# Mamba states by half of the channels, with B and C fetched once per half, and a PSUM bank moved from the state sums to the expert blocks

## The chip, the cores and the metric

The kernel runs on one core of one Trainium2 chip, in one launch. The metric is the device time of the execution in microseconds (us). A core has five engines with a queue of instructions each: PE (TensorE, matrix products), DVE (VectorE), ACT (ScalarE), POOL (GpSimd) and SP (SyncE, which here issues transfers). Each engine works through its queue in order; waits between engines are semaphores. Transfers run on 16 DMA engines. PE writes its results into PSUM, which has eight banks of 512 float32 values per partition.

## The reference, cut to what matters

The input is 16 sequences of 512 tokens with 128 features. Six residual steps follow each other, each on a layer-normalized input: half of an expert layer (8 experts, 2 chosen per token, with a capacity), attention, half of that expert layer again, half of a second expert layer, a Mamba mixer, and half of the second expert layer again.

```
x = x + 0.5 * _L0_ffn_ref(_layernorm(x), ...)
x = x + _L0_attn_ref(_layernorm(x), ...)
x = x + 0.5 * _L0_ffn_ref(_layernorm(x), ...)
x = x + 0.5 * _L1_ffn_ref(_layernorm(x), ...)
x = x + _L1_attn_ref(_layernorm(x), ...)      # Mamba
x = x + 0.5 * _L1_ffn_ref(_layernorm(x), ...)
```

The change touches Mamba's scan. For each of 256 channels d and 16 states n, along the 512 tokens:

```
dA = exp(delta[t, d] * A[d, n])
h  = h * dA + delta[t, d] * B[t, n] * x[t, d]
y[t, d] = sum over n of h[d, n] * C[t, n]
y = (y + D * x) * silu(z), then the product with W_out
```

B and C depend on the token and the state, but not on the channel. An expert block is two products with a GELU between: h = gelu(x W1 + b1), y = h W2 + b2.

## The kernel before, in words

**Layout.** All activations (`x_0` to `x_15`, one tile per sequence) stay in SBUF. The work of the six steps is cut into tasks per sequence or per group of sequences. All arithmetic is float32.

**Expert layers.** A call of an expert layer works on a group of 2 to 5 sequences. `front` normalizes and computes the gate, `routes` chooses experts and slots on DVE, `scatter` writes each token's row to its two slots in DRAM with indirect transfers from POOL, `blocks` runs the experts on blocks of 256 slots, and `back` gathers each token's two results with indirect transfers and adds them. There are 16 calls and 368 blocks. A block is: SP loads the weights `wb` (578 KB, three buffers, L693) and the rows `xs` (128 KB, three buffers, L697); PE transposes the rows into PSUM (`turned`, L709) and DVE or ACT copies them out as `bl_xT` (L712, L714); PE does the first product into two banks `ps_h` (L727); ACT applies the GELU into `hT` (L736); PE does the second product into `ps_b` (L676); DVE adds the bias into `yo` (L681), and the ACT queue issues the store (L685). The second product of a block is issued one block later than its first. Transposes and second products both take their bank from the pool `ps_b`, which holds one.

**Attention.** Two sequences may be in work at a time. For each of four tiles of 128 queries: scores into `ps_a` (two banks), mask and maximum on DVE, exponent on ACT, transposes into `ps_s0` (L867), a copy by ACT (L869), the product with v into `ps_s1` (L872) and the addition into x on DVE (L875). The projection to v also goes into `ps_s1` (L843).

**Mamba.** The 256 channels are two halves (h = 0, 1) of 128 partitions, the 16 states are eight pairs (g). `before` does the projections and convolutions, `delta` makes delta, its product `dx` with x, and writes the rows of B and C to DRAM. `states` runs over g outside and h inside. Once per g, SP loads a pair of rows of B and of C, spread over all partitions (512 KB each, L969; B has two buffers, C three). Then one step per (g, h): DVE multiplies B with `dx` into `u` (L978); for each of the two states ACT computes the exponent into a bank of `ps_a` (L984) and DVE scans along the tokens (L987); POOL multiplies with C (L990); and PE adds the result to the sum of the half, as a product with the identity (L997). The sums of both halves are open over all eight g, in two banks, `ps_s0` and `ps_s1`. `u` has five buffers. There are 16 x 16 = 256 steps. `end` adds D times x to both sums (L1010), multiplies with the gate (L1013), and does the output product (L1017).

**Order.** The program text doesn't set the order of the instructions. A planner at the end of the kernel function first picks among the tasks by ranks and due times, running each to its next `yield`; then `arrange` takes the resulting stream and gives each engine its own order by a list schedule with written-in costs of the instructions and the transfers, the number of buffers in each pool, and the order in which each pool's tiles were asked for. That order is fixed in the built program. A change of buffers therefore moves instructions everywhere.

PSUM is full: `ps_h` 2 banks, `ps_b` 1, `ps_t` 1, `ps_s` 2, `ps_a` 2.

Of the kernel before, what the change touches and what calls it, by code (L numbers as in the profile page):

```python
# [11 lines left out]
F32 = mybir.dt.float32  # L12
I32 = mybir.dt.int32
AF = mybir.ActivationFunctionType
ALU = mybir.AluOpType
AX = mybir.AxisListType
PSUM = bass.MemoryType.PSUM

P = 128
NB, SEQ, D = 16, 512, 128  # L20
NT = SEQ // P
# [6 lines left out]
DI, NH = 256, 2  # L28
NS = 16
RANK = 64  # L30
NCH = 2
# [285 lines left out]
def macaron_kernel(ctx: ExitStack, tc: tile.TileContext, a: dict, out: bass.AP):  # L317
    nc = tc.nc

    def pool(name, bufs, **kw):  # L320
        return ctx.enter_context(tc.tile_pool(name=name, bufs=bufs, **kw))
# [11 lines left out]
    bc_p = pool("bc", 3)  # L333
    s_p = pool("scan", 5)
    dram = pool("dram", 2, space=bass.MemoryType.DRAM)
    ps_h = pool("ps_h", 1, space=PSUM)
    ps_b = pool("ps_b", 1, space=PSUM)
    ps_t = pool("ps_t", 1, space=PSUM)
    ps_s = pool("ps_s", 1, space=PSUM)
    ps_a = pool("ps_a", 2, space=PSUM)  # L340
# [10 lines left out]
    def load(name, src, shape):  # L351
        t = const.tile(shape, F32, name=name)
        nc.scalar.dma_start(out=t, in_=src)
        return t
# [14 lines left out]
    dp = load("dp", a["L1_attn_D_param"], [P, NH])  # L369
# [5 lines left out]
    for e in range(E):  # L375
# [5 lines left out]
        out=tril, in_=ones, compare_op=ALU.is_ge, fill=0.0, base=0, pattern=[[-1, P]],  # L381
# [4 lines left out]
        out=upper, in_=ones, compare_op=ALU.is_gt, fill=0.0, base=0, pattern=[[1, P]],  # L386
# [15 lines left out]
    for g in range(NSLOTS):  # L402
        t = dram.tile([NBLK * BS, D], F32, name=f"slots_{g}", bufs=1)
# [9 lines left out]
    for pre, names in (("L0_ffn_", ("W1", "W2", "b1", "b2")), ("L1_ffn_", ("w1", "w2", "b1", "b2"))):  # L413
        t = dram.tile([P, E, WIDE], F32, name=f"packed_{pre}", bufs=1)
        w1d, w2d, b1d, b2d = (a[pre + n] for n in names)
        at = 0
        for src in (w1d, w2d.rearrange("p e f d -> p e (f d)"), b1d, b2d.unsqueeze(0).to_broadcast([P, E, D])):
            n = src.shape[2]
# [74 lines left out]
    def transpose(src, psum):  # L493

        for j in range(NT):
            nc.tensor.transpose(psum[:, j * P : (j + 1) * P], src[:, j, :], ident)
# [327 lines left out]
    def attention(b):  # L824
        scale = D ** -0.5
        xn = normalized(x[b])
        pt = ps_a.tile([P, SEQ], F32, name="ps_a")
        transpose(xn, pt)
        xT = xT_p.tile([D, PAD + SEQ], F32, name="xT")[:, :SEQ]
        nc.scalar.copy(xT, pt)  # L830
        yield
        qk = []
        both = m_p.tile([P, 2, SEQ], F32, name="a_qk", tag=f"cv{b % 2}")
        for i, n in enumerate("qk"):
            pq = ps_a.tile([P, SEQ], F32, name="ps_a")
            nc.tensor.matmul(pq, wa[n], xT, start=True, stop=True)
            t = both[:, i, :]
            nc.scalar.copy(t, pq)
            qk.append(t)
        q, k = qk  # L840
        pv = ps_s.tile([P, NT, D], F32, name="ps_s1")
        for j in range(NT):
            nc.tensor.matmul(pv[:, j, :], xT[:, j * P : (j + 1) * P], wa["v"], start=True, stop=True)  # L843
        v = m_p.tile([P, NH, SEQ], F32, name="a_v", tag="dx", bufs=2)[:, 0, :].rearrange(
            "p (j d) -> p j d", j=NT
        )
        nc.scalar.copy(v, pv)
        yield
        for i in range(NT):
            n = (i + 1) * P  # L850
            s = ps_a.tile([P, SEQ], F32, name="ps_a")
            nc.tensor.matmul(s[:, :n], q[:, i * P : n], k[:, :n], start=True, stop=True)
            nc.vector.tensor_tensor(s[:, i * P : n], s[:, i * P : n], tril, ALU.mult)

            m = m_p.tile([P, NH, SEQ], F32, name="a_m", tag="zs", bufs=3)[:, 0, :]
            nc.vector.tensor_scalar(m[:, :n], s[:, :n], 0.0, HIDDEN, ALU.is_equal, ALU.mult)
            nc.vector.tensor_tensor(m[:, :n], m[:, :n], s[:, :n], ALU.add)
            g = small.tile([P, 1], F32, name="a_g")
            nc.vector.tensor_reduce(g, m[:, :n], AX.X, ALU.max)
            nc.vector.tensor_scalar(g, g, LEAST, -scale, ALU.max, ALU.mult)  # L860
            pr = m_p.tile([P, NH, SEQ], F32, name="a_p", tag="xc", bufs=3)[:, 0, :]
            z = small.tile([P, 1], F32, name="a_z")
            nc.scalar.activation(pr[:, :n], m[:, :n], AF.Exp, bias=g, scale=scale, accum_out=z)
            nc.vector.reciprocal(z, z)
            pp = ps_s.tile([P, SEQ], F32, name="ps_s0")
            for j in range(i + 1):
                nc.tensor.transpose(pp[:, j * P : (j + 1) * P], pr[:, j * P : (j + 1) * P], ident)  # L867
            pT = m_p.tile([P, NH, SEQ], F32, name="a_pT", tag="dl", bufs=2)[:, 0, :]
            nc.scalar.copy(pT[:, :n], pp[:, :n])  # L869
            po = ps_s.tile([P, SEQ], F32, name="ps_s1")[:, :D]  # L870
            for j in range(i + 1):
                nc.tensor.matmul(  # L872
                    po, pT[:, j * P : (j + 1) * P], v[:, j, :], start=j == 0, stop=j == i
                )
            nc.vector.scalar_tensor_tensor(x[b][:, i, :], po, z, x[b][:, i, :], ALU.mult, ALU.add)  # L875
            yield

    def mamba(b):
# [81 lines left out]
        def states():  # L960


            zs, xc, dl, dx, rows = (st[n] for n in ("zs", "xc", "dl", "dx", "rows"))
            py = []
            for g in range(NS // NCH):
                bc = []
                for n, name in enumerate(("B", "C")):
                    t = bc_p.tile([P, NCH, SEQ], F32, name=name, bufs=2 + n)
                    nc.sync.dma_start(  # L969
                        out=t,  # L970
                        in_=rows[n, g * NCH : (g + 1) * NCH, :]
                        .unsqueeze(0)
                        .to_broadcast([P, NCH, SEQ]),
                    )
                    bc.append(t)
                for h in range(NH):
                    u = s_p.tile([P, NCH, SEQ], F32, name="u")
                    nc.vector.tensor_tensor(  # L978
                        u, bc[0], dx[:, h, :].unsqueeze(1).to_broadcast([P, NCH, SEQ]), ALU.mult
                    )  # L980
                    for i in range(NCH):
                        n = g * NCH + i
                        da = ps_a.tile([P, SEQ], F32, name="ps_a")
                        nc.scalar.activation(  # L984
                            da, dl[:, h, :], AF.Exp, scale=am[:, h, n : n + 1]
                        )
                        nc.vector.tensor_tensor_scan(  # L987
                            u[:, i, :], da, u[:, i, :], 0.0, ALU.mult, ALU.add
                        )
                    nc.gpsimd.tensor_tensor(u, u, bc[1], ALU.mult)  # L990

                    def later(g=g, h=h, u=u):
                        if not py:
                            for n in range(NH):
                                py.append(ps_s.tile([P, SEQ], F32, name=f"ps_s{n}"))
                        for i in range(NCH):
                            nc.tensor.matmul(  # L997
                                py[h],
                                ident,
                                u[:, i, :],  # L1000
                                start=g == 0 and i == 0,
                                stop=g == NS // NCH - 1 and i == NCH - 1,
                            )

                    yield later

            def end():
                ys = xc
                for h in range(NH):
                    nc.vector.scalar_tensor_tensor(  # L1010
                        ys[:, h, :], xc[:, h, :], dp[:, h : h + 1], py[h], ALU.mult, ALU.add
                    )
                nc.vector.tensor_tensor(ys, ys, zs, ALU.mult)  # L1013
                po = ps_t.tile([P, NT, D], F32, name="ps_t")
                for j in range(NT):
                    for h in range(NH):
                        nc.tensor.matmul(  # L1017
                            po[:, j, :],
                            ys[:, h, j * P : (j + 1) * P],
                            wout[:, h, :],  # L1020
                            start=h == 0,
                            stop=h == NH - 1,
                        )
                nc.vector.tensor_tensor(x[b], x[b], po, ALU.add)

            st["end"] = end
# [20 lines left out]
    def of(n, b):  # L1047
        return next(g for g, m in enumerate(moes[n]) if b in m["members"])
# [83 lines left out]
    for b in range(NB):  # L1132
        for n in range(4):
            g = of(n, b)
# [30 lines left out]
    while left:  # L1165
        ready = []
        for name in left:
            t = tasks[name]
# [4 lines left out]
        at, _, name = min((r for r in ready if r[0] <= first + WINDOW), key=lambda r: (r[1], r[0]))  # L1173
        t = tasks[name]
# [59 lines left out]
```

## Time and profile before

| | |
|---|---|
| time, median of 3 runs | 3594.3 us (3581.81 to 3594.71) |
| profiled execution, its own time | 3629.43 us |
| span of the profile | 3627.7 us |
| PE busy | 2802.4 us (77%) |
| DVE busy | 2412.1 us (66%) |
| ACT busy | 2152.2 us (59%) |
| POOL busy | 1855.7 us (51%) |
| moved by DMA | 552.52 MB, mean 152 GB/s |
| mean granted clock of PE | 0.90 |

The profile is one execution. Busy time is the time in which an engine carries out an instruction. A group of instructions is told by its line in the kernel, its engine, its operation, and its tiles as out<-in; behind the bar stand its busy time in us and the mean duration of one in ns, behind the second bar the idle time of the engine just ahead of these instructions, with what ended it. PEld is PE's weight load. SPq is the queue of SP with its transfers. A float32 product shows as two instructions of PE. PEclk is the share of the clock that PE was granted.

### The profile page before, as it was taken

The numbers are of one execution on the slowest core, as the hardware profiler recorded it, in microseconds if no ns is written. First come the engines' busy times: TensorE is split into PE (matmuls) and PEld (weight loads), VectorE is DVE, ScalarE is ACT, GpSimd is POOL, SyncE is SP. The second block draws the span as 40 slices with busy tenths as digits, with TensorE's granted clock in tenths as the row PEclk, the third lists the DMA queues.
The fourth block names the chain that finished last, engine by engine and source line by source line (L and its number), as shares of the span: only waits on it lengthen the run. The fifth ranks groups of instructions, "written<-read, shape, count | busy, mean of one in ns | idle before, by whom it ended". The sixth has DMA issues, their size and how long they took to land. (4 is left out here: it accounts for less than half of the span.)

```text
span 3627.7 us, 45599 instructions
## 1 busy us (share of the span) xinstructions
PE 2802.4 (77%) x13384; PEld 2005.3 (55%) x13384; DVE 2412.1 (66%) x5487; ACT 2152.2 (59%) x3752; POOL 1855.7 (51%) x1557
## 2 busy tenths in 40 slices
PE   3788686776767758887897986789899679854775
PEld 2677575665656645675555652455566256521564
DVE  6714572572662418863798898889788897999512
ACT  2335372552634438873887874789788669842432
POOL 2771504405245343555636468873644984577413
PEclk9999887978889879998999997999999989977888
DMA  9675414414346535654555452455565356433354
GB/s 291 184 215 156 117 58 136 143 52 144 92 124 186 153 104 186 213 161 144 177 177 173 151 182 86 145 175 169 156 192 157 132 174 205 135 115 118 108 169 134
DMA packets 379575, 552.52 MB, mean 152 GB/s; under 512 B 43136, under 2 KB 278336, under 8 KB 379328
## 3 DMA queue, kind: packets, MB, share of 16 engines
q1 hardware_dynamic: 243648, 433.39, 38.8%
q0 software_dynamic: 32768, 67.17, 6.1%
q10 hardware_dynamic: 102912, 49.06, 4.7%
q8 instruction: 107, 1.75, 0.2%
q14 instruction: 140, 1.15, 0.1%
HBM read 448.28 MB, written 110.66 MB: 154 GB/s over the span
## 5 line engine op out<-in xcount | busy, mean ns | idle before, releaser
L990 POOL TENSOR_TENSOR u<-u,C 128x1024 f32<-128x1024 f32 x256 | 640.6, 2506 | 536.5 <-DVE u L987 367.9
L736 ACT ACTIVATE hT<-ps_h,wb 128x256 f32<-128x256 f32 x1472 | 602.4, 474 | 525.9 <-PE ps_h L727 306.6
L676 PE MATMUL ps_b<-wb,hT 128*128 128x128 f32 x5888 | 800.9, 289 | 109.7 <-DVE bl_xT L712 47.8
L676 PEld LDWEIGHTS ps_b<-wb,hT 128*128 128x128 f32 x5888 | 769.2, 203 | 208.9 <-issue 82.0
L727 PE MATMUL ps_h<-bl_xT,wb 128*128 128x256 f32 x2944 | 803.9, 405 | 26.0 <-ACT hT L736 13.8
L775 POOL DMA_INDIRECT gt<-results,whole x512 | 523.8, 1023 | 571.0 <-DVE x L767 171.3
L662 POOL DMA_INDIRECT slots<-row,whole x512 | 532.1, 1039 | 521.8 <-issue 268.6
L997 PE MATMUL ps_s<-u,ident 128*128 128x512 f32 x1024 | 553.3, 659 | 156.2 <-POOL u L990 155.8
L727 PEld LDWEIGHTS ps_h<-bl_xT,wb 128*128 128x128 f32 x2944 | 558.8, 205 | 163.7 <-issue 71.3
L987 DVE TENSOR_TENSOR_SCAN u<-ps_a,u 128x512 f32<-128x512 f32 x512 | 602.8, 1208 | 49.6 <-ACT ps_a L984 43.3
L681 DVE TENSOR_TENSOR yo<-ps_b,wb 128x256 f32<-128x256 f32 x368 | 154.4, 420 | 685.7 <-PE ps_b L676 383.8
L978 DVE TENSOR_TENSOR u<-B,dx 128x1024 f32<-128x1024 f32 x256 | 450.3, 1767 | 31.0 <-PE ps_s L997 18.5
L984 ACT ACTIVATE ps_a<-dl,am 128x512 f32<-128x512 f32 x512 | 345.2, 686 | 197.1 <-DVE u L987 173.4
L997 PEld LDWEIGHTS ps_s<-u,ident 128*128 128x128 f32 x1024 | 192.5, 206 | 362.9 <-POOL u L990 219.7
L709 PE MATMUL ps_b<-ident,xs 128*128 128x128 f32 x736 | 164.0, 298 | 237.8 <-DVE yo L681 167.1
L767 DVE SCALAR_TENSOR_TENSOR x<-gt,m,x 128x128 f32<-128x128 f32 x512 | 228.8, 455 | 80.4 <-DMA gt<-results,whole 69.5
L709 PEld LDWEIGHTS ps_b<-ident,xs 128*128 128x128 f32 x736 | 95.1, 148 | 331.7 <-DVE yo L681 212.2
L907 PE MATMUL ps_t<-xT,wc 128*128 128x512 f32 x512 | 242.3, 611 | 22.6 <-ACT cv L910 9.1
L736 ACT ACT_TABLE_LOAD x176 | 225.8, 1283 | 56.2 <-PE ps_h L727 20.5
L657 POOL TENSOR_SCALAR row<-x,q,off 128x128 f32<-128x128 f32 x256 | 157.7, 618 | 135.2 <-DVE off L564 122.6
L984 ACT ACT_TABLE_LOAD x146 | 187.3, 1283 | 13.9 <-DVE yo L681 5.4
L714 ACT ACTIVATE bl_xT<-ps_b,beta,gamma 128x256 f32<-128x256 f32 x184 | 103.3, 561 | 154.4 <-PE ps_b L709 117.9
(170 smaller groups left out, 2904.5 us busy)
## 6 DMA issues: line engine op xcount, KB each, us to landing
wb<-packed_L_ffn__215 SPq DMA_DIRECT2D x184, 578.0 KB
wb<-packed_L_ffn__222 SPq DMA_DIRECT2D x184, 578.0 KB
B<-rows SPq DMA_DIRECT2D x128, 512.0 KB
C<-rows SPq DMA_DIRECT2D x128, 512.0 KB
xs<-slots SPq DMA_DIRECT2D x368, 128.0 KB
results<-yo ACTq DMA_DIRECT2D x368, 128.0 KB
slots<-empty SPq DMA_DIRECT2D x4, 3456.0 KB
slots<-row,whole POOLq DMA_INDIRECT x512
```

Source lines behind the costliest of these rows:

```text
L662: ins = nc.gpsimd.indirect_dma_start(out=dst, out_offset=bass.IndirectOffsetOnAxis(ap=st["whole"][:, k, i : i + 1], axis=0), in_=row, in_o ...
L676: nc.tensor.matmul(py[:, j, :], hT[:, f, j * P : (j + 1) * P], w2b[:, f, :], start=f == 0, stop=f == NF - 1,)
L709: nc.tensor.transpose(pt[:, j * P : (j + 1) * P], xs[:, j, :], ident)
L727: nc.tensor.matmul(ph[f // 2][:, f % 2, :], w1b[:, f * P : (f + 1) * P], xT, start=True, stop=True)
L736: return nc.scalar.activation(hT[:, f, :], ph[f // 2][:, f % 2, :], act, bias=b1b[:, f : f + 1])
L775: nc.gpsimd.indirect_dma_start(out=gt, out_offset=None, in_=st["results"][: nblk * BS, :], in_offset=bass.IndirectOffsetOnAxis(ap=st["whol ...
L907: nc.tensor.matmul(ph, wc[i][:, h, k, :], xT[:, at : at + SEQ], start=k == 0, stop=k == 3)
L978: nc.vector.tensor_tensor(u, bc[0], dx[:, h, :].unsqueeze(1).to_broadcast([P, NCH, SEQ]), ALU.mult)
L984: nc.scalar.activation(da, dl[:, h, :], AF.Exp, scale=am[:, h, n : n + 1])
L987: nc.vector.tensor_tensor_scan(u[:, i, :], da, u[:, i, :], 0.0, ALU.mult, ALU.add)
L990: nc.gpsimd.tensor_tensor(u, u, bc[1], ALU.mult)
L997: nc.tensor.matmul(py[h], ident, u[:, i, :], start=g == 0 and i == 0, stop=g == NS // NCH - 1 and i == NCH - 1,)
```

## The change

The loops of `states` are turned round: h outside, g inside. B and C are now loaded inside both, so that each pair of rows is loaded once for each half. Only one half's sum is open at a time, in one bank `ps_s`; after the eighth g of a half its D times x is added at once, by the instruction that stood in `end`. Attention's transposes and its product with v share this one bank, and the projection to v takes a bank of `ps_a`. The pool `ps_b` gets the bank that has come free. The buffers of B, C and u are as they were, and so is the arithmetic of each step. The planner, its ranks and the costs are unchanged and give a new order.

```diff
-    ps_b = pool("ps_b", 1, space=PSUM)
+    ps_b = pool("ps_b", 2, space=PSUM)
...
-        pv = ps_s.tile([P, NT, D], F32, name="ps_s1")
+        pv = ps_a.tile([P, NT, D], F32, name="ps_a")
...
-            pp = ps_s.tile([P, SEQ], F32, name="ps_s0")
+            pp = ps_s.tile([P, SEQ], F32, name="ps_s")
...
-            po = ps_s.tile([P, SEQ], F32, name="ps_s1")[:, :D]
+            po = ps_s.tile([P, SEQ], F32, name="ps_s")[:, :D]
...
-            py = []
-            for g in range(NS // NCH):
-                bc = []
-                for n, name in enumerate(("B", "C")):
-                    t = bc_p.tile([P, NCH, SEQ], F32, name=name, bufs=2 + n)
-                    nc.sync.dma_start(...)
-                    bc.append(t)
-                for h in range(NH):
+            py = {}
+            for h in range(NH):
+                for g in range(NS // NCH):
+                    bc = []
+                    for n, name in enumerate(("B", "C")):
+                        t = bc_p.tile([P, NCH, SEQ], F32, name=name, bufs=2 + n)
+                        nc.sync.dma_start(...)
+                        bc.append(t)
                     u = s_p.tile([P, NCH, SEQ], F32, name="u")
...
                     def later(g=g, h=h, u=u):
-                        if not py:
-                            for n in range(NH):
-                                py.append(ps_s.tile([P, SEQ], F32, name=f"ps_s{n}"))
+                        if g == 0:
+                            py[h] = ps_s.tile([P, SEQ], F32, name="ps_s")
...
+                        if g == NS // NCH - 1:
+                            nc.vector.scalar_tensor_tensor(
+                                xc[:, h, :], xc[:, h, :], dp[:, h : h + 1], py[h], ALU.mult, ALU.add
+                            )
...
             def end():
                 ys = xc
-                for h in range(NH):
-                    nc.vector.scalar_tensor_tensor(
-                        ys[:, h, :], xc[:, h, :], dp[:, h : h + 1], py[h], ALU.mult, ALU.add
-                    )
```

More of the change, by code (lines that the diff above doesn't have):

```diff
@@ L963, in states @@
             zs, xc, dl, dx, rows = (st[n] for n in ("zs", "xc", "dl", "dx", "rows"))
-            py = []
-            for g in range(NS // NCH):
-                bc = []
-                for n, name in enumerate(("B", "C")):
-                    t = bc_p.tile([P, NCH, SEQ], F32, name=name, bufs=2 + n)
[L969 to L973, printed above, removed]
-                    )
-                    bc.append(t)
-                for h in range(NH):
+            py = {}
[4 more added lines that the diff above has]
+                        t = bc_p.tile([P, NCH, SEQ], F32, name=name, bufs=2 + n)
+                        nc.sync.dma_start(
+                            out=t,
+                            in_=rows[n, g * NCH : (g + 1) * NCH, :]
+                            .unsqueeze(0)
+                            .to_broadcast([P, NCH, SEQ]),
+                        )
+                        bc.append(t)
                     u = s_p.tile([P, NCH, SEQ], F32, name="u")
@@ L1003, in later @@
                             )
+                        if g == NS // NCH - 1:
+                            nc.vector.scalar_tensor_tensor(
+                                xc[:, h, :], xc[:, h, :], dp[:, h : h + 1], py[h], ALU.mult, ALU.add
+                            )
                     yield later
@@ L1008, in end @@
                 ys = xc
-                for h in range(NH):
-                    nc.vector.scalar_tensor_tensor(
-                        ys[:, h, :], xc[:, h, :], dp[:, h : h + 1], py[h], ALU.mult, ALU.add
-                    )
                 nc.vector.tensor_tensor(ys, ys, zs, ALU.mult)
```

## The prediction

> **What bounds the kernel now.** I read the table of stages first: the busy time of each engine in three stretches, cut at the first and at the last multiply with B (L978 starts at 1381.4 us and ends near 3378).
>
> ```profile
> core 0: us, PE busy (x) PEld busy (x) DVE busy (x) ACT busy (x) POOL busy (x), PEclk, DMA share, GB/s
> 0.00:1330.00 1330.00, 955.52 (x5336) 796.22 (x5337) 659.68 (x2744) 570.77 (x1241) 553.02 (x667) 0.88 0.49 145
> 1330.00:3390.00 2060.00, 1682.96 (x7040) 1067.70 (x7039) 1704.88 (x2587) 1495.63 (x2316) 1239.83 (x822) 0.91 0.50 157
> 3390.00:3628.00 238.00, 163.96 (x1012) 141.33 (x1010) 47.55 (x157) 85.81 (x196) 62.82 (x68) 0.89 0.51 151
> ```
>
> No engine is full in stage 1 (expert blocks and attention): PE leads with 955.52 of 1330 (72%). In stage 2 (Mamba, with expert blocks between) DVE has 83% and PE 82%. Stage 3 is the last 37 expert blocks, where DVE has 20%. The DMA engines stand at half everywhere.
>
> Second, what PE waits for (the view of waits, whole execution):
>
> ```profile
> PE ps_b L709 <- DVE yo L681: 167.1, 106, 11.5
> PE ps_s L997 <- POOL u L990: 155.8, 78, 14.1
> PE ps_b L709 <- issue: 48.6, 18, 17.8
> PE ps_b L676 <- DVE bl_xT L712: 47.8, 22, 10.1
> PE ps_b L676 <- ACT bl_xT L714: 19.7, 16, 5.9
> ```
>
> The columns are total us, times, longest. The first line is the one bank ps_b: the transposes of the next block (L709) wait until DVE has emptied the second product (yo). The fourth and fifth are the same bank the other way round. The second line is not about banks: POOL's product with C is late. By stage, the same view gives L709 for yo 87.7, 55.2 and 24.2 us, and L676 for bl_xT 54.3, 8.3 and 3.0.
>
> Third, the chain of DVE and the tiles B and C. L978, L987 (groups) and then the DMA rates around one pair B, C (40 slices of 0.25 us from 3350; B was issued at 3350.59, C at 3351.01):
>
> ```profile
> L987 DVE TENSOR_TENSOR_SCAN u<-ps_a,u 128x512 f32<-128x512 f32 x512 | 602.8, 1208 | 49.6 <-ACT ps_a L984 43.3
> L978 DVE TENSOR_TENSOR u<-B,dx 128x1024 f32<-128x1024 f32 x256 | 450.3, 1767 | 31.0 <-PE ps_s L997 18.5 <-issue 11.4 <-DMA xs<-slots 0.5
> DMA  0000005898896999889964200000000000007000
> ```
>
> DVE hardly ever waits for B (nothing of the 31.0 us is a B transfer). The pair's data flows from about 3351.5 to 3355.7, so the second of two tiles is there 4.7 us after its issue; one tile alone is half of that flow, some 3.2 us from issue.
>
> **The change, part by part.** The sum is made against the profiled execution, 3629.4 us (span 3627.7 and 1.7 around it); it ran 35.1 us over the median of the runs, 3594.3. I carry the difference over to the median. In the built order the blocks stay where they were (159 before the first state sum, then 172, then 37), so each part can be priced in its own stage. The order of PE does use the bank: transposes stand directly behind a second product 199 times (81 before), and the second products are cut into 686 groups (477).
>
> *Second bank of ps_b, stage 1.* The uses of ps_b alternate, so with two banks transposes always get one and second products the other. A wait of L709 for yo is not wholly removed: after the transposes (0.4 us) and a first product (1.9) PE meets the next second product, and that needs the bank which the same yo must empty. So a wait gives back at most about 2.1 us. The 49 waits of 87.7 us in this stage are mostly below 2 us with a few up to 11.5; cut at 2.1 they hold 50. Cut at 2.0, one second product, the 54.3 us of L676 hold 28. Together 78 us of PE time. PE is idle 374 us there, and the other waits (normalized rows, routing, scatters through POOL) remain, so only a part reaches the end; I take a third: **-26** (between 0 and -78).
>
> *Stage 2.* 63 us by the same lines, of which some 50 can be had; PE shares this stage with DVE, which the bank doesn't relieve. I take **-15** (0 to -50).
>
> *Stage 3.* Here the timeline repeats with a period of 4.47 us:
>
> ```profile
> 3466.07 0.44 PE L709 MATMUL ps_b<-ident,xs 128*128 128x128 f32 x2 [0.52 <-DVE yo L681]
> 3466.14 0.37 SPq L693 DMA_DIRECT2D wb<-packed_L_ffn__222  x1
> 3466.34 1.89 PE L727 MATMUL ps_h<-bl_xT,wb 128*128 128x256 f32 x8
> 3468.07 1.95 PE L676 MATMUL ps_b<-wb,hT 128*128 128x128 f32 x16
> 3480.09 1.97 PE L727 MATMUL ps_h<-bl_xT,wb 128*128 128x256 f32 x8 [0.18 <-DMA wb<-packed_L_ffn__222]
> ```
>
> 0.52 us a block for 37 blocks would be 19 us. But the weights of the block after next are requested by the same yo (3466.14), and they are needed 4.67 us later; at 3480.09 they came 0.18 us late, 5.0 after their issue. Without the 0.52 us the loads are what is late next. **-5** (0 to -19).
>
> A rule speaks against all three: the Trainium skill, "TensorE: Matmul & The Clock Gate", section "HAM oscillation — how this bites in real kernels", tells of a kernel where double-buffering PSUM gave nothing more once the array was kept busy. By it the three parts are 0; by the rows they are -46. I keep the rows, because this PE is at 72% in stage 1 and its granted clock at 0.88; but the rule is why I don't take the 78 whole.
>
> *B and C once per half.* 128 issues of each become 256. SP pays 256 x 0.32 us = 82 us, spread over 2060 us on a queue that mostly waits. The bytes: 256 x 512 KB = 134 MB more; stage 2 moves 157 GB/s at a share of 0.50, so a full share is 314 GB/s and 134 MB are 427 us, a share of 0.21: 0.50 becomes 0.71. What counts is the lead of a tile. B has two buffers. One B served two steps (h = 0, 1), so it was requested three steps ahead; now it is requested when the multiply two steps back has ended. C's three buffers cover three steps instead of six. From the timeline's starts and ends of the 256 L978, the gap from the end of one to the start of the next but one has a median of 10 us, but DVE also issues two multiplies back to back, and then it is 1 to 4 us. With B there 4.7 us after the request, 33 of 254 steps come short, by 41 us in all; at 3.5 us it is 18 steps and 13 us; at 6.6 us 59 steps and 127 us. The same count for C (POOL's product three back) gives nothing at 4.7. What waits behind L978 on DVE are the scans, yo and bl_xT, so the loss goes to PE too. The skill's page "DMA: Bandwidth & Descriptors", section "Anatomy of one DMA — SWDGE (gpsimd) path", prices a transfer at 2.0 us plus its bytes over 436 GB/s, 3.2 us for 512 KB, which agrees with one lone tile and would make this part +13; the trace's pair, 4.7, makes it +41. Every step now asks for a pair, beside weights, so: **+41** (13 to 127).
>
> *One bank of state sums.* The 16 changes of batch become 32 changes of half. At each, PE's next sum waits for L1010 (0.74 us) and for DVE to come to it, up to one L978 (1.2 to 4.0 us). 16 more changes at about 2 us are 32; five u buffers and the blocks between hide part on PE. L1010 itself waited 9.3 us in all for PE; that can double. Together **+20** (0 to 100, a full 6.3 us step each). The additions of D themselves are as many as before.
>
> *Attention.* pp and po share the one ps_s. po needs the copy of pp anyway, so only the next tile's pp waits for po's reader (L875). In the timeline pp and po occupancies overlap by 22 us in all; **+8** (0 to 22). v's product moves to ps_a, which has two banks, at no cost: L838 empties them within 0.6 us.
>
> *Other transfers under a share of 0.71.* DVE waited 12.2 us for gathered rows and PE 4.0 us for weights in stage 2; I let both double and round up: **+10** (0 to 40).
>
> Sum: -26 - 15 - 5 + 41 + 20 + 8 + 10 = **+33**: 3662 for the profiled execution, 3594 + 33 = **3627** for the median.
>
> **The rivals.**
> 1. *The bank pays (faster).* Two thirds of stage 1's 78, half of stage 2's 50, 10 in the tail, because PE leads stage 1[...]; costs at the low ends (13 + 5 + 3 + 5): 26 - 52 - 25 - 10 = -61, 3533. For it: the largest single wait of PE is this bank. Against it: weights are requested by the same yo, and half of the blocks run in a stage that DVE shares. It decides against me from the point where more than 79 of the 147 us (78 + 50 + 19) of removable PE waits reach the end, or where tiles land in 3.5 us.
> 2. *B becomes the bound of stage 2 (much slower).* Where steps follow densely (37 scans in 1400:1500, 5.4 us a step, DMA share 0.60) the new tiles add 18.5 x 0.52 MB in 100 us, 97 GB/s, for a share of 0.91. If landing goes to 6.6 us or more, +127 instead of +41, and more on gathers: 3594 + 33 + 86 + 30 = 3743. Against it: such density holds for few windows; from 3150 on, dense steps have a share of 0.45 at most.
> 3. *Cancel.* Costs of 45 against gains of 45: 3594.
>
> That the change would not do what it says is excluded by the built order above.
>
> **How the numbers follow.** Less than 0.5% (18 us) can't be told from no change. Mine 0.43 (own range 3612 to 3690), rival 1 0.33 (3490 to 3576), cancel 0.17, rival 2 0.07. Slower 0.50, same 0.17, faster 0.33. The range: 3515 leaves out the lower quarter of rival 1 (0.08), 3705 rival 2 and the top of mine (0.10).
>
> **What would show it.** Right: the line L709 <- yo gone or below 30 us; idle of L978 with B as releaser, 30 to 60 us; DMA share near 0.7 and some 680 MB in all; PE's wait for L1010 at L997 appears; stage 1 shorter by 20 to 40, stage 2 longer by 50 to 80, the tail within 6 us. Wrong: stage 1 shorter by over 60, or DVE not waiting for B, or stage 2 unchanged although the share rose.

## The result, and the profile after

The changed kernel takes **3553.1 us** (median of 4 runs, 3541.96 to 3560.04), the kernel before 3588.1 on the same chip: a ratio of **0.9894** (95% interval 0.9864 to 0.9924). It is faster by 1.1%, where 0.9% slower was forecast. The profiled execution took 3560.04 us, that of before 3629.43; the latter lay 41 us over the median of its own runs, so the difference of the two profiles (70 us) shows too much.

The table of stages of the kernel after. Its cuts stand near the first and last multiply with B and not on them, as those of before did (1330 was 51 us ahead of the first multiply, although the prediction says that it cuts there):

```profile
core 0: us, PE busy (x) PEld busy (x) DVE busy (x) ACT busy (x) POOL busy (x), PEclk, DMA share, GB/s
0.00:1284.00 1284.00, 953.97 (x5331) 795.74 (x5331) 654.40 (x2744) 564.61 (x1233) 551.39 (x667) 0.89 0.51 150
1284.00:3324.00 2040.00, 1678.61 (x7024) 1065.10 (x7022) 1704.31 (x2585) 1487.92 (x2309) 1229.27 (x817) 0.91 0.70 225
3324.00:3558.00 234.00, 166.27 (x1032) 146.29 (x1032) 51.32 (x159) 91.97 (x207) 67.84 (x74) 0.89 0.53 157
```

Busy times are nearly the same in every stage. Cut at the starts of the first and last multiply themselves, the stages are 1334, 1982 and 242 us, against 1381, 1991 and 256 before: 48, 8 and 14 us shorter. The DMA share of the second rose from 0.50 to 0.70, as worked out, and yet that stage is not longer. PE's waits (total, times, longest; rows left out are marked):

```profile
PE ps_s L996 <- POOL u L990: 147.1, 69, 12.9
PE ps_b L676 <- DVE yo L681: 96.7, 68, 11.7
PE ps_b L676 <- issue: 51.2, 25, 22.1
...
PE ps_b L709 <- DVE bl_xT L712: 20.3, 7, 7.7
PE ps_h L727 <- DMA wb<-packed_L_ffn__215: 18.3, 19, 2.2
...
PE ps_s L996 <- DVE xc L1004: 13.9, 8, 3.5
...
PE ps_h L727 <- DMA wb<-packed_L_ffn__222: 13.0, 16, 1.8
```

Three rows of the kernel before, for comparison:

```profile
PE ps_b L676 <- DVE yo L681: 11.1, 18, 1.4
...
PE ps_h L727 <- DMA wb<-packed_L_ffn__222: 4.6, 9, 0.8
PE ps_h L727 <- DMA wb<-packed_L_ffn__215: 4.4, 7, 1.0
```

L709's wait for yo (167.1 us before) is gone from the head of the list. Part of it stands at L676 now, 96.7 for the same yo (11.1 before), and PE waits more for the weights, 31 us against 9. L996 for L1004 is the wait at the change of half. The groups of the scan, from the page:

```profile
L990 POOL TENSOR_TENSOR u<-u,C 128x1024 f32<-128x1024 f32 x256 | 643.0, 2515 | 518.3 <-DVE u L987 287.4
...
L987 DVE TENSOR_TENSOR_SCAN u<-ps_a,u 128x512 f32<-128x512 f32 x512 | 603.0, 1208 | 41.0 <-ACT ps_a L984 34.0
...
L978 DVE TENSOR_TENSOR u<-B,dx 128x1024 f32<-128x1024 f32 x256 | 446.0, 1748 | 37.7 <-DMA B<-rows 14.7
...
B<-rows SPq DMA_DIRECT2D x256, 512.0 KB
```

DVE waits 14.7 us for B where I had 41.

Of the signs that the prediction named, four of those for it came: L709's wait for yo is down to 4.0 us, the DMA share is 0.70, 687 MB are moved, and the wait at the change of half appears. The idle time for B (30 to 60 us forecast) and the lengths of the first two stages did not come out, and one sign of being wrong did: Mamba's stage is not longer although the share rose.

### The profile page after: what moved, and what is told of

Its sections match the earlier page's. It is cut to its first block, busy times and chain, and to the rows that moved or that the text cites. A ratio compares the mean times of both kernels' runs of the same rounds, so it can differ in the third digit from the quotient of the medians.

```text
span 3558.0 us, 46179 instructions
## 1 busy us (share of the span) xinstructions
PE 2798.8 (79%) x13384; PEld 2007.1 (56%) x13384; DVE 2410.0 (68%) x5487; ACT 2144.5 (60%) x3748; POOL 1848.5 (52%) x1557
## 3 DMA queue, kind: packets, MB, share of 16 engines
q8 instruction: 107, 1.75, 0.2%
## 5 line engine op out<-in xcount | busy, mean ns | idle before, releaser
L676 PE MATMUL ps_b<-wb,hT 128*128 128x128 f32 x5888 | 824.3, 286 | 200.0 <-DVE yo L681 96.7
L676 PEld LDWEIGHTS ps_b<-wb,hT 128*128 128x128 f32 x5888 | 781.2, 200 | 316.9 <-issue 157.2
L727 PE MATMUL ps_h<-bl_xT,wb 128*128 128x256 f32 x2944 | 790.9, 404 | 48.3 <-DMA wb<-packed_L_ffn__215 18.3
L996 PE MATMUL ps_s<-u,ident 128*128 128x512 f32 x1024 | 563.2, 672 | 161.5 <-POOL u L990 147.1
L978 DVE TENSOR_TENSOR u<-B,dx 128x1024 f32<-128x1024 f32 x256 | 446.0, 1748 | 37.7 <-DMA B<-rows 14.7
L996 PEld LDWEIGHTS ps_s<-u,ident 128*128 128x128 f32 x1024 | 194.8, 210 | 386.5 <-POOL u L990 211.9
L767 DVE SCALAR_TENSOR_TENSOR x<-gt,m,x 128x128 f32<-128x128 f32 x512 | 239.6, 479 | 80.4 <-DMA gt<-results,whole 66.3
L709 PE MATMUL ps_b<-ident,xs 128*128 128x128 f32 x736 | 153.6, 286 | 61.2 <-DVE bl_xT L712 20.3
L907 PEld LDWEIGHTS ps_t<-xT,wc 128*128 128x128 f32 x512 | 98.6, 198 | 142.2 <-issue 106.7
L479 ACT ACTIVATE xn<-x,off,q 128x128 f32<-128x128 f32 x256 | 106.2, 484 | 108.8 <-DVE off L564 89.2
```

What stands on the lines that cost most here:

```text
L676: nc.tensor.matmul(py[:, j, :], hT[:, f, j * P : (j + 1) * P], w2b[:, f, :], start=f == 0, stop=f == NF - 1,)
L727: nc.tensor.matmul(ph[f // 2][:, f % 2, :], w1b[:, f * P : (f + 1) * P], xT, start=True, stop=True)
L767: nc.vector.scalar_tensor_tensor(xj, gt, st["weight"][k][:, i : i + 1], xj, ALU.mult, ALU.add)
L907: nc.tensor.matmul(ph, wc[i][:, h, k, :], xT[:, at : at + SEQ], start=k == 0, stop=k == 3)
L978: nc.vector.tensor_tensor(u, bc[0], dx[:, h, :].unsqueeze(1).to_broadcast([P, NCH, SEQ]), ALU.mult)
L996: nc.tensor.matmul(py[h], ident, u[:, i, :], start=g == 0 and i == 0, stop=g == NS // NCH - 1 and i == NCH - 1,)
```

## The experiments

Times in this part are compared on one chip only, each with runs of the kernel before beside it: that kernel takes 3367 to 3377 us on some chips and 3588 to 3621 on others (more on this at the end). One per cent is 34 to 36 us.

**The kernel before, profiled again.** No edit.

> The kernel before, unchanged, profiled once more: the one profile of before ran 3629 us, 41 us over the median of its runs, so the 70 us between the two profiles can't all be the change. Expected: a profile of 3585 to 3600 us, of which the first stage (to the first multiply with B) takes some 1365 us instead of 1381, the tail some 250.

3373.6 us, on a chip where before has a median of 3369.0. It shows the chip, not the profile: the first stage, up to the first L978, is 1187 us instead of 1381.

**The parts of the change.** `turn_only` turns the loops and leaves the banks as they were:

```diff
-    ps_b = pool("ps_b", 2, space=PSUM)
+    ps_b = pool("ps_b", 1, space=PSUM)
...
-                            py[h] = ps_s.tile([P, SEQ], F32, name="ps_s")
+                            py[h] = ps_s.tile([P, SEQ], F32, name=f"ps_s{h}")
```

(against the kernel after; attention as before).

> The loops are turned (h outside, B and C fetched per half, D times x added per half), but the two halves keep a bank each, attention keeps its two banks and ps_b has one. My forecast's terms for this: +41 for tiles that come late, +10 for other transfers, nothing for the banks, so +50 us (1.4% slower). Rival, what the profile after suggests (DVE waits only 14.7 us for B, POOL 30.7 for C): +0 to +20, within 0.5%. Second rival: the turned loop is itself a gain, since one half's steps follow each other: -15 or more.

1.0139 of before (1.0114 to 1.0164), 3417.3 us: 48 us, my +50 as a sum. That is chance: the cause that I had priced, the fetching, comes to about 14 us in `fetch_twice` below. `one_sum_bank` is the whole change with `pool("ps_b", 1)`:

> As the change, but ps_b keeps one bank; the freed bank lies idle. All of the change's costs without its gain. My forecast: +41 +20 +8 +10 = +79 us (2.2% slower). Rival (transfers hidden, half changes hidden): +0 to +25. The second bank's worth is then the change minus this: -46 by my forecast, which with the measured -38 would make this +8; by a rival in which the bank is worth twice what I took, this is +55.

1.0157 (1.0131 to 1.0183), and again beside the next two runs:

> The change with ps_b at one bank, now on the chip of the change. If its ratio of 1.0157 holds here, the second bank is worth 2.7% in all (some 97 us), twice what I took, against costs of 56 us instead of 79. If costs are smaller here, near 1.00 to 1.005, the bank is worth about 1.5% (54 us), close to my 46, and the costs were what I overrated.

1.0175 (1.0155 to 1.0194), 3424.5 us. The one bank of sums and attention's sharing thus add some 0.2% to `turn_only`, within the intervals, where I had 0.8%; the planner orders each of these kernels anew, so the small difference can also be that of two orders. `fetch_twice` keeps the loops of before and only moves the loads of B and C into the inner one:

```diff
-                bc = []
-                for n, name in enumerate(("B", "C")):
...
-                for h in range(NH):
+                for h in range(NH):
+                    bc = []
+                    for n, name in enumerate(("B", "C")):
```

> The kernel before with its loops as they were (g outside, both sums open, one bank of ps_b), but B and C are fetched in the inner loop, once for each half: only the bytes and the shorter lead of B and C change. My forecast's terms for it were +41 and +10, 1.4%. If what turn_only lost (1.4%) is the fetching, this is 1.010 to 1.018 of before; if it is the order of steps by half, it is within 0.5%.

1.0039 (1.0020 to 1.0058), 3381.3 against 3367.1 us: 14 us, of which the new order that the planner makes can be a part. It lies within the 0.5% that were expected if the loss of `turn_only` is not in the fetching. DVE waits 13.0 us for B there.

**The waits and the order apart.** `plan_one_bank` has two banks of ps_b, but the planner is told one, so that every engine has the order of `one_sum_bank`, instruction for instruction:

```diff
-    free = {tag: [0.0] * q[0].tag_meta.bufs for tag, q in queue.items()}
+    free = {tag: [0.0] * (1 if q[0].name.startswith("ps_b") else q[0].tag_meta.bufs) for tag, q in queue.items()}
```

> The change with two banks of ps_b, but its planner is told that there is one: every engine has exactly the order of one_sum_bank, and only the waits at run time differ. If the bank's gain is the waits that fall away in a given order (what I priced, at most 2.1 us each), this is as fast as the change, about -46 us against one_sum_bank. If the gain is in the order that the planner can make with two banks (second products split, transposes earlier), this is within 15 us of one_sum_bank.

> Two banks, one_sum_bank's order held. If the two causes are as the earlier runs on two chips read together: about midway, 1.25% under one_sum_bank and 1.4% over the change. If the order is worth nothing: equal to the change within 0.3%. If the waits are worth nothing: equal to one_sum_bank.

1.0030 (1.0018 to 1.0043) and, on the next chip, 1.0028 (1.0014 to 1.0042). The change beside the latter:

> The change once more, as the measure for the two that follow, all on one chip: 0.987 to 0.989 of before.

0.9887 (0.9866 to 0.9908). On that one chip the medians are 3424.5 (one bank), 3377.6 (two banks, order held), 3332.6 us (two banks, order planned for them): **46.9 us for the waits, 45.0 us for the order**. On the chip of `plan_one_bank` and `one_sum_bank` the waits come to 44.8 us. PE's waits in the three, first one bank:

```profile
PE ps_b L709 <- DVE yo L681: 103.9, 123, 4.1
...
PE ps_b L676 <- DVE bl_xT L712: 42.3, 27, 5.9
...
PE ps_b L676 <- DVE yo L681: 16.0, 21, 2.4
...
PE ps_h L727 <- DMA wb<-packed_L_ffn__222: 6.6, 12, 1.3
PE ps_h L727 <- DMA wb<-packed_L_ffn__215: 6.0, 10, 1.1
```

two banks, order held:

```profile
PE ps_b L676 <- DVE yo L681: 34.3, 25, 4.9
PE ps_h L727 <- DMA wb<-packed_L_ffn__215: 29.7, 34, 2.5
...
PE ps_h L727 <- DMA wb<-packed_L_ffn__222: 20.3, 21, 2.2
...
PE ps_b L709 <- DVE yo L681: 2.1, 7, 0.3
```

two banks, order planned for two:

```profile
PE ps_b L676 <- DVE yo L681: 58.1, 78, 4.0
...
PE ps_h L727 <- DMA wb<-packed_L_ffn__222: 18.7, 21, 2.9
...
PE ps_h L727 <- DMA wb<-packed_L_ffn__215: 17.7, 18, 2.5
...
PE ps_b L709 <- DVE yo L681: 3.1, 4, 2.5
```

With the order held, 102 us of L709's wait go, and the 42 of L676 for bl_xT; 18 come back at L676 for yo and 37 as weights that are late. That fits the chain that I argued for the tail (the same yo frees the bank and the weights), here in all stages: the waits for weights rise by 19.5, 8.9 and 8.9 us. The starts of the first and last L978 and the spans cut these kernels into stages:

| profile, us | to first L978 | first to last L978 | rest |
|---|---|---|---|
| before (`ctl_before`) | 1186.8 | 1951.1 | 234.0 |
| `fetch_twice` | 1189.7 | 1959.5 | 232.5 |
| `turn_only` | 1179.8 | 1997.5 | 229.2 |
| `one_sum_bank_2` | 1193.8 | 1999.8 | 229.1 |
| `plan_one_bank_2` | 1170.1 | 1979.8 | 221.2 |
| `after_3` | 1166.4 | 1949.7 | 221.2 |

In this pair of profiles the removed waits give 24, 20 and 8 us (I had 26, 15 and 5); in that of `one_sum_bank` and `plan_one_bank` on the other chip 16, 12 and 8. The order gives 4, 30 and 0 here, nearly all in Mamba's stage; these are single profiles, with 34 us between them where the medians have 45. Other draws below do not repeat this split.

**What the bytes cost.** In `few_bytes` each load of B and C for the second half fetches 128 tokens and these are read four times over (left out: the other 384 tokens, so that half computes with wrong B and C). All orders are those of the change. The edit, cut to the loads:

```diff
+                        w = SEQ if h == 0 else SEQ // 4
                         nc.sync.dma_start(
-                            out=t,
-                            in_=rows[n, g * NCH : (g + 1) * NCH, :]
+                            out=t[:, :, :w],
+                            in_=rows[n, g * NCH : (g + 1) * NCH, :w]
...
+                        bc.append(t[:, :, :w].unsqueeze(2).to_broadcast([P, NCH, SEQ // w, w]))
```

> The change with the order of every engine held, but each B and C of the second half of the channels is loaded with its first 128 tokens only and read four times over (left out: the other three quarters of these loads, so states of the second half are computed from wrong B and C). As many transfers, waits and instructions, 101 MB less moved. My forecast's terms for late tiles and other transfers, +41 and +10, should fall away for the most part: 30 to 50 us under the change. Rival: bytes are hidden, and what turning the loops costs (1.4%) is the shorter lead of B and the order of the steps: within 10 us of the change.

> The change, unchanged, beside the other three: the runs so far of the change and of its parts come from two chips on which the kernel before takes 3588 and 3369 us. If the chip makes no difference to the ratio: 0.989 of before, so 1.3% under the same kernel in its one-bank order (plan_one_bank, 1.003). If the first chip's longer stalls had favoured the change: 0.995 to 1.00.

The change: 0.9866 (0.9840 to 0.9892), 3547.1 us; with fewer bytes 0.9836 (0.9811 to 0.9861), 3540.4. The stretch from the first to the last multiply with B, `few_bytes`:

```profile
core 0: us, PE busy (x) PEld busy (x) DVE busy (x) ACT busy (x) POOL busy (x), PEclk, DMA share, GB/s
1328.00:3303.00 1975.00, 1621.20 (x6798) 1032.94 (x6796) 1684.96 (x2552) 1449.42 (x2246) 1221.44 (x811) 0.91 0.57 176
```

and the change beside it:

```profile
core 0: us, PE busy (x) PEld busy (x) DVE busy (x) ACT busy (x) POOL busy (x), PEclk, DMA share, GB/s
1319.00:3296.00 1977.00, 1630.64 (x6799) 1036.13 (x6797) 1679.17 (x2553) 1448.75 (x2246) 1221.81 (x811) 0.91 0.70 227
```

With a share of 0.57 or of 0.70 this stage has the same length within 2 us. That is what the rival said (bytes are hidden), and not the 30 to 50 us that I expected; the 7 us between the medians are within the intervals.

**Pieces of second products.** In `whole_products` the planner takes the eight products of one second product as one piece (364 groups on PE, 686 in the change); the edit, cut to its middle:

```diff
+        if ops and out.startswith("ps_b") and not i.is_transpose and product == out:
+            ops[-1].members.append(i)
+            continue
```

> The change, but the planner takes the eight products of a block's second product as one piece, so it can't put other work between them (364 groups in the built order instead of 686). If the gain that the planner's order brings (plan_one_bank to the change, about 1.3%, 45 us) lies in cutting second products into pieces, this loses it: 40 us or more over the change. If it lies in the earlier place of transposes and second products, within 15 us of the change.

0.9890 (0.9863 to 0.9916), 3555.0 us, 8 over the change and within the intervals. In its trace transposes stand directly behind a second product 82 times, as before (81), and not 199 times as in the change. So the gain in total hangs neither on cutting the second products nor on that place of the transposes. Where it falls does change: the stages of this profile are 1312, 2000 and 234 us, against 1319, 1975 and 241 of the change on the same chip. What Mamba's stage loses here, 24 us, the other two make good by 15.

**A third buffer of B**, for the fifth of u (`bufs=3` for both B and C, `pool("scan", 4)`):

> The change with a third buffer for B, paid with the fifth buffer of u. If B's lead of two steps costs what I forecast (+41 us), this is 20 us or more under the change, and DVE's wait for B falls from 15 us to near nothing; if the lead costs little, as the profile after says, it is within 10 us, or slower by the missing buffer of u.

0.9909 (0.9885 to 0.9933), 3568.1 us: 21 us slower than the change. No wait of DVE for B is left in the profile, and there is no gain to be seen; L978's wait for a sum of PE, which gives back a buffer of u, rose from 8.3 us to 21.4. The order is also another one, so the lead of B is not measured alone here.

**Is the order's gain a draw?** Any edit gives another list schedule. One cost in the planner, the delay of a signal, was set from 0.04 us to 0.03 and to 0.05 (`SIGNAL = 0.03`), for one bank, two banks and the kernel before.

> one_sum_bank with the planner's delay of a signal at 0.03 instead of 0.04 us: a neutral edit that gives another order. If orders for one bank are all worse in the Mamba stage, it stays at 1.012 to 1.022 of before. If one_sum_bank had a poor draw, it comes out near 1.00 to 1.008.

> The same with 0.05 us: 1.012 to 1.022 if the loss belongs to one bank with turned loops, 1.00 to 1.008 if it was a draw.

> The change with 0.03 us. If the better order belongs to the second bank, it stays at 0.984 to 0.994 of before; if the change had a lucky draw, it comes out near 1.00, like plan_one_bank.

> The change with 0.05 us: 0.984 to 0.994 if the order's gain belongs to the bank, near 1.00 if it was a draw.

> The kernel before with the planner's delay of a signal at 0.03 instead of 0.04 us. If its order is a typical one: within 0.4% of before, and the loss of the turned loops is real. If it is a good draw: 1.005 or more, and up to that much of turn_only's loss is the draw.

> The same with 0.05 us: 0.996 to 1.004 if typical, 1.005 or more if the order of before is a good draw.

| ratio to before | 0.04 | 0.03 | 0.05 | mean |
|---|---|---|---|---|
| before | 1 | 1.0114 (1.0085 to 1.0142) | 1.0026 (1.0011 to 1.0041) | 1.005 |
| one bank (`one_sum_bank`) | 1.0157, 1.0175 | 1.0113 (1.0091 to 1.0135) | 1.0112 (1.0091 to 1.0133) | 1.013 |
| two banks (the change) | 0.9894, 0.9866, 0.9887 | 0.9938 (0.9914 to 0.9962) | 0.9916 (0.9893 to 0.9938) | 0.991 |

An edit that means nothing moves the kernel before by up to 1.1%. So the 45 us of the order are not one firm number. The two groups stay apart in all draws, by 1.7 to 3.1%, 2.2% in the mean (79 us of 3600); that the second bank makes the kernel faster is thus no draw. The waits in a held order are 1.3 to 1.5% (47 us). If they are worth as much in the other orders, which was not run, some 0.8% (about 30 us of 3600) is left to the order as a property of the second bank, and the rest of the 45 was a good draw of the change or a poor one of `one_sum_bank`. With three orders each, and one bank at 0.04 run on the faster chips alone and at 0.03 and 0.05 on a slower one, this 0.8% is an estimate. In the same way, turned loops on one bank cost 0.8% against the mean of the orders of before (30 us), not the 1.6 to 1.75% of the single comparison.

The stages of the other draws, cut as in the table above:

| profile, us | to first L978 | first to last L978 | rest |
|---|---|---|---|
| one bank, 0.03 (`one_s03`) | 1404.3 | 2011.6 | 258.8 |
| two banks, 0.03 (`two_s03`) | 1365.0 | 1991.8 | 241.1 |
| one bank, 0.05 (`one_s05`) | 1401.3 | 2021.7 | 259.6 |
| two banks, 0.05 (`two_s05`) | 1332.3 | 2007.1 | 243.3 |

Here the second bank takes 20 and 15 us off Mamba's stage, where the pair above took 50, and not more than the 12 to 20 that the waits alone gave there; the larger part falls ahead of Mamba, 39 and 69 us, on a chip of the slower kind. So these draws show no gain of the order in Mamba's stage.

## Why the prediction was wrong

**The step that failed** is the one that priced the bank "in its own stage" in waits alone. I had seen that the built order uses the bank (transposes directly behind a second product 199 times against 81, 686 groups instead of 477) and still put the new order at nothing, on the ground that the blocks keep their places. On the chip that ran all three kernels the forecast of +79 for the costs and -46 for the bank stands against +57.3 for the costs, -46.9 for the waits and -45.0 for the order, -34.6 in all. Of the 68 us between +33 and this, 45 are the order and 22 are costs that I rated too high. Without the order, the parts as measured come to +9.8 and +10.4 us (`plan_one_bank` on two chips): 0.3% slower, and the new order turns that into 1.1% faster. Over the draws the order is worth some 30 us, by estimate. What in the new order does it is not settled, and neither is where: one pair of profiles has it in Mamba's stage, the other draws do not, and the two features of the order that I had counted are not needed for it (`whole_products`).

**The waits**, -46, came out at 46.9 and 44.8 us. The mechanism, a bank that the same yo empties so that a part of each wait comes back, is the one that the held order shows. That the sum fits so well is in part luck: a third of what could be had was a guess, and I priced it from a profile with 167.1 us at L709 on a chip of the slower kind, while the held order ran on chips where that row has 98.5 us (`ctl_before`). By stage the two pairs differ from each other by 8 us.

**Fetching twice**, +41 and +10: mis-sized. `fetch_twice` measured 14 us, `few_bytes` 7, within its intervals, for three quarters of the bytes of one half. I chose the landing of a pair, 4.7 us; the count with 3.5 us gave +13. I preferred the pair because every step now asks for two tiles. DVE waited 14.7, 13.0 and 11.7 us for B in `after`, `fetch_twice` and `after_3`, which speaks for the smaller size; that the total agrees too may be luck, since the order of `fetch_twice` is new. Two things in the working were wrong. The +13 belongs to 3.5 us and not to the 3.2 that stand beside it, which give 8.5 by the same count (7 steps). And those 3.2 us are an estimate: the Trainium skill's "DMA: Bandwidth & Descriptors", section "Anatomy of one DMA — SWDGE (gpsimd) path", prices transfers that gpsimd issues, while SP issues B and C; no run here timed the landing of one of these tiles alone. Why the pair's 4.7 us overstates the loss was not tested.

**Turned loops**, no price: the order of steps by half was not among my costs. `turn_only` lost 48 us, of which `fetch_twice` explains 14. Against the spread of orders (before with the delay at 0.03 has 1984 us in Mamba's stage, 1951 with 0.04) the rest can be a draw; this stays open.

**One bank of sums and attention**, +20 and +8: mis-sized, 0.2%, some 6 us (`one_sum_bank` against `turn_only`, 3423.6 and 3417.3 us), no more than two orders can differ by. The wait at the change of half, L996 for L1004, is there with 13.9 us.

**Stage 3**: right in kind. A part of its waits becomes late weights (2.6 to 11.5 us in this stage, `one_sum_bank_2` to `plan_one_bank_2`), and 8 us were gained where I had 5 of a possible 19.

**Stage 2** of the bank's waits was read 2 us short: L676 for bl_xT has 8.3 us for ACT and 2.0 for DVE there. It changes nothing in the argument.

**The rule on PSUM.** What I called a rule is, in the Trainium skill's "TensorE: Matmul & The Clock Gate", section "HAM oscillation — how this bites in real kernels", the measurement of one matrix-product kernel, in which double-buffering PSUM gave no further gain. The section doesn't say that this holds for others, and it doesn't carry over: two banks in an unchanged order gave 1.3 to 1.5% here.

**The range** (3515 to 3705) held the time, 3553, but the sign did not come out. Missing in the sum was a term that no view of one profile shows: how far the time moves by a new order alone, measured now at 0.3 to 1.1%.

## What to carry to other kernels

Where a planner in the program orders the instructions, a buffer has two prices: the waits that it removes in the present order, which the profile bounds and a run with the order held measures, and the order that it allows, for which no view of the profile before gave a price here. Tell them apart by giving the hardware the buffer and not the planner. Before a change of 1% is believed or explained, move one planner constant that means nothing, in both kernels, and look at how far each moves by itself.

## What the runs showed of the hardware

The same built kernel takes 3367 to 3377 us on some chips and 3588 to 3621 on others, 6 to 7%, while the ratio of the change holds on both kinds (0.9887 against 0.9866 and 0.9894). The chips with the longer times show waits for which the view names no instruction or transfer of the core as the end, "remote". The view of waits of the kernel before on the first chip:

```profile
DVE yo L681 <- remote: 184.0, 26, 16.6
...
ACT hT L736 <- remote: 57.6, 16, 17.0
...
ACT L736 <- remote: 12.1, 1, 12.1
```

On the faster chip the same view of `ctl_before` has no such row. So it is in all profiles of this document: the ten from chips with the longer time have 295 to 436 us of such waits over all engines, the ten from the others none. Of the kernel before, most of the difference lies ahead of Mamba (1381 against 1187 us). What these waits are, the traces do not say.
